# A graph layer that lives on gathers: idle writes on GpSimd behind every twentieth gather, a longer ring and shorter terms

## Chip, cores and metric

The kernel runs on one core of one Trainium2 chip. The metric is the device time of one execution in microseconds. Five engines run their own queues: TensorE (PE, with its weight loads as PEld), VectorE (DVE), ScalarE (ACT), GpSimd (POOL) and SyncE (SP, which only issues transfers here).

## What is computed

Two relational graph layers over 50,000 nodes of 128 features and 850,000 edges sorted by destination (16 relations, 8 bases), then a residual and a layer norm. 50,000 of the edges are each node's own loop edge.

```python
def _rgcn_layer(h, src, dst, rel, basis, w_comp, loop_w, bias):
    W = jnp.einsum('rb,bio->rio', w_comp, basis)
    seg = dst * N_REL + rel
    agg = segment_sum(h[src], seg, num_segments=N_ENT * N_REL).reshape(N_ENT, N_REL, -1)
    msg = jnp.einsum('nri,rio->no', agg, W)
    return jax.nn.relu(msg + h @ loop_w + bias)

h = _rgcn_layer(x, src, dst, rel, basis1, w_comp1, loop_w1, bias1)
h = _rgcn_layer(h, src, dst, rel, basis2, w_comp2, loop_w2, bias2)
out = layernorm(x + h)
```

## The kernel before

**Tiles and chunks.** At the start of the first layer the edges are closed up into 800,000 real edges (the loop edges are taken out and handled apart) and cut into 6250 tiles of 128. Ten tiles are a chunk (K = 10), so a layer has 625 chunks (C). Each tile needs 128 rows of h, one for each edge. GpSimd fetches them with one indirect transfer, `gather` (L178), into one of `RING * PER` = 30 places `g0` to `g29`; `row_of(t)` says which one, `fetch` issues five at a time, 30 tiles ahead of their use. The second layer gathers from `H1`, which the first layer has written.

**On TensorE**, a tile's rows are multiplied (L982) by `hot`, a 128x96 matrix that VectorE makes (L872): it sorts the edges of the tile into 12 nearby destinations and weighs them for the 8 bases. Five tiles share a PSUM bank `pa`; ScalarE copies it (L998) into `aT`. The second to last product of five carries the wait for the fifth gather. Four chunks later `aT` is multiplied by the bases (L741), turned, spread over four neighbours (L724) and added into the nodes' sums with `own` masks (L764, L785).

**Weights.** `hot` needs for each edge its relation's 8 coefficients. `weights(c)` makes them for chunks c and c + 1 together: `told_apart` compares relations (every fourth chunk), `summed_over` multiplies (L596) into `terms`, a sum over the 16 relations (L625) goes to the PSUM tile `fixed`. The generator has two steps for a pair of chunks; `beside` takes one step behind the tile t = 5 and one behind t = 8 of every even chunk. `loop_weights` does the same for the loop edges of four groups of nodes (L658).

**Order.** The order on PE, GpSimd, VectorE and ScalarE is written out by hand: the loop over chunks issues products, gathers and copies, and `beside` puts steps of the other work between the ten tiles of a chunk. The iotas of the kernel before (L134, L204, L223, L230 at the start, L521 at the end of the first layer's gathers) make tables of counted columns. L355 and L410 are indirect scatters of the tables of edges, also on GpSimd, in the first layer.

Of the kernel before, what the change touches and what calls it, by code (L numbers as in the profile page):

```python
# [39 lines left out]
F32 = mybir.dt.float32  # L40
# [5 lines left out]
OP = mybir.AluOpType  # L46
AX = mybir.AxisListType
# [3 lines left out]
P = 128  # L51
# [3 lines left out]
K = P // WN  # L55
# [10 lines left out]
Q = AT // 2  # L66
BANK = 512
WEIGHTS = AT * PER * 8
BITS_AT_ONCE = BANK - WEIGHTS
RING = 6  # L70
J = 4
NEAR = 128
BATCH = 4
# [10 lines left out]
def tile_rgcn_resnorm(  # L84
# [15 lines left out]
    nc = tc.nc  # L100
    N, D = x.shape
    NR, NB = w_comp1.shape
    E = edges.shape[1] // 3
    R, M = -(-E // RUN), E - N
    C = -(-M // (K * P))
# [25 lines left out]
    consts = ctx.enter_context(tc.tile_pool(name="consts", bufs=1))  # L131
# [45 lines left out]
    def gather(to, of, idx):  # L177
        return nc.gpsimd.indirect_dma_start(  # L178
            out=to, out_offset=None, in_=of, in_offset=bass.IndirectOffsetOnAxis(ap=idx, axis=0)
        )  # L180
# [11 lines left out]
        return bass.AP(tensor=edges.tensor, offset=edges.offset + j * E + first, ap=ap)  # L192


    rows = [consts.tile([P, D], F32, name=f"g{i}") for i in range(RING * PER)]
    src = consts.tile([P, 2 * C * HALF], I32, name="src")
    key = consts.tile([P, 2 * C * HALF], U8, name="key")
# [371 lines left out]
    def chunked():  # L569
        with (  # L570
# [5 lines left out]
            def ks(c):  # L576
                return min(K, -(-M // P) - c * K)
# [14 lines left out]

            def summed_over(kinds, k):

                terms = hp.tile([P, 2 * K, NB, NR], F32, name="terms", bufs=1)[:, :k]
                nc.vector.tensor_tensor(  # L596
                    terms,
                    kinds[:, :, None, :].to_broadcast([P, k, NB, NR]),
                    table[:, None, :, :].to_broadcast([P, k, NB, NR]),
                    op=OP.mult,  # L600
                )
                return terms

            def told_apart(of, by, width, c, name):

                k = sum(ks(i) for i in range(c, min(c + Q, C)))
                apart = hp.tile([P, Q * K, width], U8, name=name, bufs=1)[:, :k]
                nc.vector.tensor_tensor(
                    apart,
                    of[:, None, :width].to_broadcast([P, k, width]),  # L610
                    by[:, c * K : c * K + k, None].to_broadcast([P, k, width]),
                    op=OP.is_equal,
                )
                return apart

            def weights(c):

                if c % Q == 0:
                    kinds_of[0] = told_apart(of_rel, rel, NR, c, "kinds")
                at = c % Q * K  # L620
                k = ks(c) + (ks(c + 1) if c + 1 < C else 0)
                terms = summed_over(kinds_of[0][:, at : at + k], k)
                yield
                pm = fixed[:, : 2 * K * NB].rearrange("p (k b) -> p k b", b=NB)
                nc.vector.tensor_reduce(pm[:, :k], terms, AX.X, OP.add)  # L625
                weighed_for[c] = pm[:, :K]
                weighed_for[c + 1] = pm[:, K:]
                yield

            def loop_weights(g, n):  # L630

                few = min(T, NGR - g)
                which_rel = hp.tile([P, 2, T, J], I32, name="lrel", bufs=1)
                for h in range(2):
                    nc.sync.dma_start(
                        which_rel[:, h, :few, :],
                        bass.AP(
                            tensor=LREL.tensor,
                            offset=LREL.offset + h * NL + g * GN,
                            ap=[[J, P], [GN, few], [1, J]],  # L640
                        ),
                    )
                yield
                both = hp.tile([P, 2, T * J, NR], U8, name="both_kinds", bufs=1)
                for h in range(2):
                    nc.vector.tensor_tensor(
                        both[:, h, : few * J],
                        of_rel[:, None, 1 : NR + 1].to_broadcast([P, few * J, NR]),
                        which_rel[:, h].rearrange("p t j -> p (t j)")[:, : few * J, None].to_broadcast([P, few * J, NR]),
                        op=OP.is_equal,  # L650
                    )
                nc.vector.tensor_tensor(
                    both[:, 0, : few * J], both[:, 0, : few * J], both[:, 1, : few * J], op=OP.add
                )
                yield
                terms = summed_over(both[:, 0, : few * J], few * J)
                lw = hp.tile([P, T * J, NB], F32, name="lw")
                nc.vector.tensor_reduce(lw[:, : few * J], terms, AX.X, OP.add)  # L658
                yield lw.rearrange("p (t j) b -> p j t b", t=T)

            def from_itself(g, of, n):
# [157 lines left out]
            def done(steps):  # L819
                for _ in steps:  # L820
                    pass
# [38 lines left out]
            for n, of in enumerate((x, H1)):  # L860

                weighed_for, kinds_of, own_of = {}, [None], [None]
# [22 lines left out]
                def added_in(c):  # L885

                    if c < ALONE:
                        return [c - LAG] if c >= LAG else []
                    at = ALONE - LAG + 2 * (c - ALONE)
                    return list(range(at, min(at + 2, C)))  # L890
# [14 lines left out]
                def add(c):  # L905

                    for g in to_nodes(c, n):
                        assert made[0] > g
                        ending.append(finish(g, n))

                def beside(t, c, owning, summing, weighing):

                    if c % 2 == 0 and t in (5, 8):
                        next(weighing, None)
                    if t in (4, 9) or c >= ALONE - 3 and t in (0, 2):
                        next(owning, None)
                    if c < ALONE:
                        if t in (1, 3, 6, 9):
                            next(summing, None)
                    elif c == ALONE:  # L920
                        for _ in range(2):
                            next(summing, None)
                    elif t == (1 if c == C - 1 else 2):
                        done(summing)
                    if t in (2, 6, 9) and ending:
                        if next(ending[0], 0) == 0:
                            ending.pop(0)
                    if t == (4 if c == C - 1 else 5 if c == ALONE else 8):
                        for one in added_in(c):
                            add(one)  # L930
# [3 lines left out]
                def row_of(t):  # L934

                    turn, k = divmod(n * tiles + t, RING * PER)
                    return rows[k if turn % 2 == 0 else k // PER * PER + PER - 1 - k % PER]

                def fetch(some):

                    for t in some:
                        if t < tiles:
                            fetched[t] = gather(row_of(t), of, src[:, t : t + 1]).ins

                fetched = {}
                now, made = [0], [0]
                owning = own_of_all()
                for c in range(C):
# [6 lines left out]
                    if c == 0:  # L955
                        fetch(range(RING * PER))
                        nc.vector.tensor_copy(table, COMP[n].rearrange("p r b -> p b r"))
                        weighing = weights(0)
                        done(weighing)
                        hots[0] = hot_of(0)  # L960
                        hots[1] = hot_of(1)
                        if n == 0:
                            for _ in range(LBITS + 3):
                                next(first_runs)
                    if c % 2 == 0 and c + 2 < C:
                        weighing = weights(c + 2)
# [9 lines left out]
                    for k in range(0, K, PER):  # L976
                        m = min(PER, ks(c) - k)
                        if m > 0:
                            pa = ps_a.tile([P, BANK], F32, name="pa")
                        for i in range(PER):  # L980
# [12 lines left out]
                            if i == m - 1:  # L993
                                at = c * K + k + RING * PER
                                fetch(range(at, at + PER))
# [28 lines left out]
    def summed():  # L1024
        L1 = dram.tile([N, D], F32, name="L1")
        L2 = dram.tile([N, D], F32, name="L2")
        with tc.tile_pool(name="io", bufs=2) as io, tc.tile_pool(name="sbf", bufs=2) as sb:
# [140 lines left out]
            nodes(L2, norm, also=x)  # L1168

    chunked()  # L1170
    wrong = nc.values_load(bad[0:1, 0:1], min_val=0, max_val=1)
    with tc.If(wrong > 0):
# [7 lines left out]
def build(arrays):  # L1180
    import concourse.bacc as _bacc

    nc = _bacc.Bacc("TRN2", target_bir_lowering=False, num_devices=1)
    args = [
        nc.dram_tensor(name, a.shape, mybir.dt.from_np(a.dtype), kind="ExternalInput").ap()
        for name, a in arrays.items()
    ]
    args.append(nc.dram_tensor("out_0_dram", arrays["in_x_dram"].shape, F32, kind="ExternalOutput").ap())
    with tile.TileContext(nc) as tc:
        tile_rgcn_resnorm(tc, *args)  # L1190
    return nc
# [21 lines left out]
```

## Times and profile before

| | |
|---|---|
| median of 3 runs | 15732.13 us (15731.26 to 15733.83) |
| profiled execution, its own time | 15732.04 us |
| its span, from the first to the last instruction | 15730.2 us |
| mean granted TensorE clock | 0.816 |
| busy: PE, DVE, ACT, POOL | 74%, 65%, 12%, 75% of the span |
| gathers | 12,500, two layers of 6250 |

The span is what the trace covers; the time of an execution is 1.8 us more. A row of a group gives the line, the engine, the operation and its tiles (out<-in) with shapes, then the count, the busy time in all (us) and the mean of one (ns), and behind the last bar the idle time of that engine just before them with what ended it. "issue" means that the engine waited for nothing that the profile shows.

### The profile page before, as it was taken

The page shows a single profiled execution, that of the slowest core. Times are in us where ns is not written, and L with a number is a line of the kernel's source. Part 1 is how long each engine was busy: PE and PEld are TensorE (multiplying, and loading weights), DVE is VectorE, ACT ScalarE, POOL GpSimd, SP SyncE. Part 2 cuts the span into 40 slices and gives each one's busy share as a digit, 9 for nine tenths or more (in the row PEclk, how much of TensorE's full clock was granted, in tenths as well). Part 3 has the DMA queues.
Part 4 walks back from the last instruction along what each step waited for, and adds up shares of the span by engine and source line. Part 5 has one row for each costly group of instructions (what it writes and reads, how often), then busy time and mean ns, then how long its engine had stood idle before and what let it go on. Part 6 is the DMA issues. An engine that isn't in the chain of part 4 may idle for free.

```text
span 15730.2 us, 119374 instructions
## 1 busy us (share of the span) xinstructions
PE 11573.8 (74%) x41202; PEld 7067.3 (45%) x41202; DVE 10159.2 (65%) x10480; ACT 1936.8 (12%) x3683; POOL 11853.5 (75%) x12532
## 2 busy tenths in 40 slices
PE   6777777777777777777777777777777777777777
PEld 4444444444444444444444444444444444444444
DVE  8767776777655566556666666666666666666666
ACT  1111111111111111111111111111111111111111
POOL 7777777777777777777777777777777777777777
PEclk8888888888888888888878888888888888878888
DMA  2222222222222222222222222222222222222222
GB/s 83 71 71 67 72 65 71 68 67 70 62 60 60 60 60 60 60 60 60 60 58 64 62 63 62 63 63 63 63 63 63 63 62 63 63 63 63 62 63 61
DMA packets 539213, 1004.82 MB, mean 64 GB/s; under 512 B 261489, under 2 KB 264561, under 8 KB 538612
## 3 DMA queue, kind: packets, MB, share of 16 engines
q0 software_dynamic: 401872, 826.89, 18.4%
q1 hardware_dynamic: 133652, 168.42, 3.4%
q8 instruction: 343, 5.62, 0.1%
q14 instruction: 258, 2.11, 0.0%
q10 hardware_dynamic: 3088, 1.79, 0.0%
HBM read 924.65 MB, written 71.59 MB: 63 GB/s over the span
## 4 chain that ended last, share of the span: by engine, by line
POOL 21%; DMA 11%; issue 10%; PE 8%; DVE 0%; POOLq 0%; ACT 0%; DVEq 0%
POOL g L178 21%; DMA g<-H,src 11%; PE pn L785 3%; PE po L741 3%; PE pa L982 1%; PE po L691 1%; DVE ls L706 0%; PE po L713 0%; PE pn L795 0%; DVE by L698 0%; DVE slots L724 0%; DVE fixed L625 0%; POOLq L178 0%; DVE hot L872 0%; DVE terms L596 0%
## 5 line engine op out<-in xcount | busy, mean ns | idle before, releaser
L982 PE MATMUL pa<-hot,g 128*128 128x96 f32 x25000 | 4897.9, 314 | 4005.0 <-DMA g<-in_x_dram,src 1947.1
L178 POOL DMA_INDIRECT g<-in_x_dram,src x6250 | 5927.2, 948 | 1912.2 <-issue 1643.2
L178 POOL DMA_INDIRECT g<-H,src x6250 | 5902.0, 944 | 1918.5 <-issue 1650.9
L982 PEld LDWEIGHTS pa<-hot,g 128*128 128x128 f32 x25000 | 4305.7, 222 | 6622.5 <-issue 4200.4
L698 DVE TENSOR_TENSOR by<-po,lw 128x512 f32<-128x512 f32 x1568 | 1074.8, 686 | 3926.2 <-PE po L691 3925.4
L785 PE MATMUL pn<-slots,own 120*128 120x512 f32 x4128 | 3193.6, 908 | 63.4 <-DVE own L764 35.0
L998 ACT COPY aT<-pa 128x480 f32<-128x480 f32 x2500 | 1393.6, 557 | 10593.6 <-PE pa L982 10592.0
L741 PE MATMUL po<-aT,basis 128*128 128x480 f32 x4960 | 2162.0, 591 | 0.0
L691 PE MATMUL po<-basis,hT 128*128 128x512 f32 x3136 | 1991.6, 722 | 19.4 <-DVE by L698 16.0
L625 DVE TENSOR_REDUCE fixed<-terms 128x160 f32<-128x2560 f32 x626 | 1764.2, 2818 | 10.2
L596 DVE TENSOR_TENSOR terms<-kinds,fixed 128x2560 f32<-128x2560 uint8 x626 | 1760.0, 2812 | 11.1
L706 DVE TENSOR_REDUCE ls<-by 128x128 f32<-128x1152 f32 (+1 forms) x784 | 1660.3, 2118 | 32.9
L872 DVE TENSOR_TENSOR hot<-fixed,own 128x960 f32<-128x960 f32 x1250 | 1437.8, 1150 | 33.3 <-PE pa L982 16.5
L741 PEld LDWEIGHTS po<-aT,basis 128*128 128x128 f32 x4960 | 966.3, 200 | 984.9 <-issue 984.9
L785 PEld LDWEIGHTS pn<-slots,own 120*128 120x128 f32 x4128 | 1022.6, 278 | 766.8 <-issue 691.3
L724 DVE TENSOR_TENSOR slots<-po,which 120x1024 f32<-120x1024 f32 (+1 forms) x630 | 761.7, 1209 | 541.1 <-PE po L750 513.2
L691 PEld LDWEIGHTS po<-basis,hT 128*128 128x128 f32 x3136 | 581.7, 231 | 25.1 <-DVE by L698 16.9
L745 ACT COPY by_slot<-po 128x480 f32<-128x480 f32 x310 | 173.0, 558 | 2545.1 <-PE po L741 2545.1
L764 DVE TENSOR_SCALAR own<-col,node 120x256 f32<-120x256 f32 (+1 forms) x1250 | 438.1, 351 | 8.1 <-PE pn L785 8.1
L807 DVE TENSOR_TENSOR pn<-pn,ls 128x512 f32<-128x512 f32 x98 | 68.0, 694 | 477.2 <-PE pn L785 477.2
L795 PEld LDWEIGHTS pn<-loop,hT 128*128 128x128 f32 x1568 | 294.9, 262 | 169.3 <-issue 169.3
L807 DVE TENSOR_TENSOR ls<-pn,ls 128x512 f32<-128x512 f32 x98 | 67.2, 685 | 403.4 <-PE pn L785 403.4
(137 smaller groups left out, 3185.4 us busy)
## 6 DMA issues: line engine op xcount, KB each, us to landing
g<-in_x_dram,src POOLq DMA_INDIRECT x6250, 2.5
g<-H,src POOLq DMA_INDIRECT x6250, 2.5
h_own<-in_x_dram SPq DMA_DIRECT2D x97, 256.0 KB, 2.7
xw<-in_x_dram SPq DMA_DIRECT2D x97, 256.0 KB, 2.7
H<-ls SPq DMA_DIRECT2D x97, 256.0 KB, 2.1
h_own<-H SPq DMA_DIRECT2D x97, 256.0 KB, 2.7
out_dram<-ls SPq DMA_DIRECT2D x97, 256.0 KB, 2.4
FULL<-full SPq DMA_DIRECT2D x20, 640.0 KB, 4.5
```

Source lines behind the costliest of these rows:

```text
L178: return nc.gpsimd.indirect_dma_start(out=to, out_offset=None, in_=of, in_offset=bass.IndirectOffsetOnAxis(ap=idx, axis=0))
L596: nc.vector.tensor_tensor(terms, kinds[:, :, None, :].to_broadcast([P, k, NB, NR]), table[:, None, :, :].to_broadcast([P, k, NB, NR]), op= ...
L625: nc.vector.tensor_reduce(pm[:, :k], terms, AX.X, OP.add)
L691: nc.tensor.matmul(hb[:m], hT[:, j, :m], BASIS[n][:, b : b + few, :].rearrange("p b d -> p (b d)"), start=True, stop=True,)
L698: nc.vector.tensor_tensor(by[:m, b : b + few, :], hb[:m].rearrange("p (b d) -> p b d", d=D), lw[:m, j, g % T, b : b + few, None].to_broadc ...
L706: nc.vector.tensor_reduce(ls[:m, j, :], by[:m].rearrange("p b d -> p d b"), AX.X, OP.add)
L724: nc.vector.tensor_tensor(to[:k], of[:k, :, None, :].to_broadcast([k, pair, J, D]), which[:k, c : c + pair, :, None].to_broadcast([k, pair ...
L741: nc.tensor.matmul(ps[:, : BATCH * S], BASIS[n][:, b, :], aT[:, b, :], start=b == 0, stop=b == NB - 1)
L785: nc.tensor.matmul(sums[g], own, of[:k].rearrange("s j d -> s (j d)"), start=c == first(g), stop=c == final(g),)
L872: nc.vector.tensor_tensor(hot[:, : ks(c)], pm[:, : ks(c), :, None].to_broadcast([P, ks(c), NB, WN]), own[:, : ks(c), None, :].to_broadcast ...
L982: product = nc.tensor.matmul(pa[:, i * NB * WN : (i + 1) * NB * WN], row_of(c * K + k + i), hot[:, k + i].rearrange("e b w -> e (b w)"), s ...
L998: nc.scalar.copy(aT[:, :, place_of + k * WN : place_of + (k + m) * WN].rearrange("d b (i w) -> d i b w", w=WN), pa[:, : m * NB * WN].rearr ...
```

## The change

Four edits. Behind every twentieth gather of a layer (t + 1 divisible by 2K) GpSimd writes the counted columns 0 to 639 twice into `lull`, a tile of 128x640 that nothing reads. The ring has 7 x 5 = 35 places, so gathers are issued 35 tiles ahead. `weights` makes product and sum for each chunk of a pair alone, in four steps, and `beside` takes a step behind t = 5 and t = 8 of every chunk. `terms` is half as wide, and `loop_weights` goes through its 16 rows in pieces of ten and six. In SBUF, `lull` (2560 bytes a partition) and five more places (2560 bytes) stand against half of `terms` (5120 bytes).

```diff
-RING = 6
+RING = 7
+IDLE = 640
...
+    lull = consts.tile([P, IDLE], F32, name="lull")
     rows = [consts.tile([P, D], F32, name=f"g{i}") for i in range(RING * PER)]
...
-                terms = hp.tile([P, 2 * K, NB, NR], F32, name="terms", bufs=1)[:, :k]
+                terms = hp.tile([P, K, NB, NR], F32, name="terms", bufs=1)[:, :k]
...
-                at = c % Q * K
-                k = ks(c) + (ks(c + 1) if c + 1 < C else 0)
-                terms = summed_over(kinds_of[0][:, at : at + k], k)
-                yield
                 pm = fixed[:, : 2 * K * NB].rearrange("p (k b) -> p k b", b=NB)
-                nc.vector.tensor_reduce(pm[:, :k], terms, AX.X, OP.add)
-                weighed_for[c] = pm[:, :K]
-                weighed_for[c + 1] = pm[:, K:]
-                yield
+                for i in range(c, min(c + 2, C)):
+                    at, to = i % Q * K, pm[:, (i - c) * K : (i - c + 1) * K]
+                    terms = summed_over(kinds_of[0][:, at : at + ks(i)], ks(i))
+                    yield
+                    nc.vector.tensor_reduce(to[:, : ks(i)], terms, AX.X, OP.add)
+                    weighed_for[i] = to
+                    yield
...
-                terms = summed_over(both[:, 0, : few * J], few * J)
                 lw = hp.tile([P, T * J, NB], F32, name="lw")
-                nc.vector.tensor_reduce(lw[:, : few * J], terms, AX.X, OP.add)
+                for k in range(0, few * J, K):
+                    m = min(K, few * J - k)
+                    terms = summed_over(both[:, 0, k : k + m], m)
+                    nc.vector.tensor_reduce(lw[:, k : k + m], terms, AX.X, OP.add)
...
-                    if c % 2 == 0 and t in (5, 8):
+                    if t in (5, 8):
                         next(weighing, None)
...
                             fetched[t] = gather(row_of(t), of, src[:, t : t + 1]).ins
+                            if (t + 1) % (2 * K) == 0:
+                                for _ in range(2):
+                                    nc.gpsimd.iota(
+                                        lull,
+                                        pattern=[[1, IDLE]],
+                                        base=0,
+                                        channel_multiplier=0,
+                                        allow_small_or_imprecise_dtypes=True,
+                                    )
```

## The prediction

> **What bounds the kernel now.** I read the page first (engine totals, the chain, the groups), then GpSimd's own waits, then its timeline where something interrupts its stream. Columns of a group: count, then busy us and mean ns of one, then idle time before them and what ended it.
>
> ```profile
> span 15730.2 us, 119374 instructions
> PE 11573.8 (74%) x41202; PEld 7067.3 (45%) x41202; DVE 10159.2 (65%) x10480; ACT 1936.8 (12%) x3683; POOL 11853.5 (75%) x12532
> POOL 21%; DMA 11%; issue 10%; PE 8%; DVE 0%; POOLq 0%; ACT 0%; DVEq 0%
> L982 PE MATMUL pa<-hot,g 128*128 128x96 f32 x25000 | 4897.9, 314 | 4005.0 <-DMA g<-in_x_dram,src 1947.1
> L178 POOL DMA_INDIRECT g<-in_x_dram,src x6250 | 5927.2, 948 | 1912.2 <-issue 1643.2
> L178 POOL DMA_INDIRECT g<-H,src x6250 | 5902.0, 944 | 1918.5 <-issue 1650.9
> ```
>
> No engine is above 75% and the chain splits over four names, so the shares alone name no limit. The two L178 rows do. Busy and idle together, the 12,500 gathers fill 5927.2 + 1912.2 + 5902.0 + 1918.5 = 15659.9 us of the 15730.2. What is that idle time? GpSimd's waits (total us, times, longest us):
>
> ```profile
> POOL g L178 <- issue: 3294.1, 10764, 14.0
> POOL g L178 <- DMA g<-in_x_dram,src: 189.3, 621, 0.3
> POOL g L178 <- DMA g<-H,src: 184.7, 606, 0.3
> POOL g L178 <- PE pa L982: 101.5, 333, 0.3
> ```
>
> Whatever is named, a wait is 0.3 us: 189.3/621 = 0.305, 101.5/333 = 0.305, and (3294.1 - 14.0)/10763 = 0.305. It is a constant step between two gathers, and the releaser is only whatever happened to occur inside it; the chain's "DMA" and "issue" are partly this step too. So a gather costs 0.944 + 0.305 = 1.249 us, and 12,500 of them 15,613 us. That is the kernel: GpSimd never waits for a free place nor for TensorE, while TensorE waits for gathers. The rest is the start, the step between the layers and the tail. GpSimd's timeline at the step between the layers (start, duration, in brackets the idle time before):
>
> ```profile
> 7886.79 0.94 POOL L178 DMA_INDIRECT g<-in_x_dram,src  x1 [0.30 <-issue]
> 7887.75 0.65 POOL L521 IOTA even<- 1x625 f32 x1
> 7902.45 0.95 POOL L178 DMA_INDIRECT g<-H,src  x1 [14.05 <-issue]
> 7903.70 0.95 POOL L178 DMA_INDIRECT g<-H,src  x1 [0.30 <-issue]
> 7904.96 0.94 POOL L178 DMA_INDIRECT g<-H,src  x1 [0.30 <-issue]
> 7906.20 0.94 POOL L178 DMA_INDIRECT g<-H,src  x1 [0.30 <-issue]
> ```
>
> Two things are to be seen. An iota queued behind a gather starts when that gather ends (7886.79 + 0.94 = 7887.73, start 7887.75): it does not run beside it. And after a pause of 14 us the gathers go on at 1.25 us each: rest is not paid back by a faster pace.
>
> **The change, part by part.**
>
> *The lulls.* A layer has 6250 gathers; the condition holds at every 20th, so 312 times a layer, 624 times in all, with 1248 iotas of 128x640. The trace has iotas of nearby sizes, alone and one behind the other at the start:
>
> ```profile
> L223 POOL IOTA place<- 128x672 f32 x1 | 0.7, 687 | 0.0
> L521 POOL IOTA even<- 1x625 f32 x1 | 0.7, 652 | 0.0
> L204 POOL IOTA col<- 128x256 f32 x1 | 0.3, 334 | 0.0
> ```
> ```profile
> 1.52 0.69 POOL L223 IOTA place<- 128x672 f32 x1
> 2.17 0.40 POOL L230 IOTA spread<- 5x120 f32 x2
> ```
>
> A column costs (687 - 334)/(672 - 256) = 0.849 ns, so 640 columns cost 687 - 32 x 0.849 = 660 ns. L521, met in the middle of the gathers, gives 652 + 15 x 0.849 = 665, so gathers before it do not slow an iota. An iota behind an iota starts 2.17 - 1.52 = 0.65 us after it, 0.04 ahead of its recorded end. A lull then lasts, from the end of its gather, 0.02 + (0.66 - 0.04) + 0.66 = 1.30 us.
>
> What comes after is not in the trace: no gather follows an iota without a wait for something else. Either the 0.30 us step still stands between the last iota and the next gather, and the lull adds 1.30 + 0.30 - 0.30 = 1.30 us; or the step runs under the iotas, and it adds 1.00. Below that I see no way: the iotas themselves have to run. The nearest row is an indirect transfer that was released by VectorE after GpSimd had been idle for 18 us:
>
> ```profile
> 19.66 0.89 DVE L353 SCALAR_TENSOR_TENSOR full<-both,run_first,real 128x640 f32<-128x640 f32 x1
> 20.84 1.14 POOL L355 DMA_INDIRECT FULL<-full,to_i  x1 [18.27 <-DVE full L353]
> ```
>
> Its release is at 19.66 + 0.89 = 20.55 and it starts 0.29 us later, though the engine had had all the time to prepare it. So the step comes after whatever lets the instruction go, and should come after an iota too; since a successor can start 0.04 us ahead of an iota's recorded end, I take 0.26 to 0.30, that is 1.26 to 1.30, and 1.28 as the value. 624 x 1.28 = 799 us. With the step hidden it is 624 x 1.00 = 624 us.
>
> All of it lies on the path: the stream of gathers has no slack in which a lull could lie, and the last lulls of each layer stand 10 gathers before its end. Behind a lull are queued the next gathers, in the first layer also the few scatters of the run tables; TensorE waits for the gathers.
>
> *35 places.* A gather may run 35 instead of 30 ahead. No wait of GpSimd above 0.305 us was for a place, so this takes nothing off: 0. Should a lull let TensorE fall behind, the five places are cover, not gain. At the very start five more gathers stand before the first scatter of the loop relations, 5 x 1.25 = 6 us and one lull more; that delays VectorE once, not GpSimd.
>
> *Terms for single chunks.* One product and one sum over 2560 columns become two of each over 1280. Both shapes are in the trace, since the last chunk has no partner:
>
> ```profile
> L625 DVE TENSOR_REDUCE fixed<-terms 128x160 f32<-128x2560 f32 x624 | 1761.2, 2822 | 10.2
> L596 DVE TENSOR_TENSOR terms<-kinds,fixed 128x2560 f32<-128x2560 uint8 x624 | 1757.0, 2816 | 11.0
> L625 DVE TENSOR_REDUCE fixed<-terms 128x80 f32<-128x1280 f32 x2 | 3.0, 1495 | 0.1
> L596 DVE TENSOR_TENSOR terms<-kinds,fixed 128x1280 f32<-128x1280 uint8 x2 | 3.0, 1486 | 0.1
> ```
>
> The pair costs 2 x 1486 - 2816 = 156 ns and 2 x 1495 - 2822 = 168 ns more, together 324 ns x 624 = 202 us of VectorE; the loop's terms, 48 of 2048 columns now cut in two, add some 15 us by the same step. VectorE is busy 10159 of 15730 us, and two chunks (20 gathers, 25 us) hold 16 us of its work, so 0.35 us more is hidden by its idle time, and the work is spread more evenly over odd and even chunks. Without that cover it would be 217 us. A weight is now finished one chunk before its use is prepared instead of two, in the same chunk as the product that needs it and ahead of it in VectorE's order: 0.
>
> *Sum.* The profiled execution took 15732.04 us with its span of 15730.2; the median of the three runs, 15732.13, is the same. 15732 + 799 = **16531 us**, 5.1% more.
>
> **A rule weighed.** The transfers themselves, by the page's queues and issues:
>
> ```profile
> q0 software_dynamic: 401872, 826.89, 18.4%
> g<-H,src POOLq DMA_INDIRECT x6250, 2.5
> ```
>
> A gather lands 2.5 us after its issue, two gathers' distance, and the queue takes 18.4% of the transfer engines: nothing piles up there, and the pace is that of GpSimd's own instructions. The Trainium skill, DMA: Bandwidth & Descriptors, section Anatomy of one DMA, puts most of the fixed 2 us of such a transfer on completion and calls the generation of descriptors small; by that rule issuing would not be the limit and the time would stay. The rows do not bear it out for a stream of gathers: 1.249 us of each are GpSimd's.
>
> A second rule speaks for more than my sum. VectorE's masks beside a gather:
>
> ```profile
> 9178.53 0.35 DVE L764 TENSOR_SCALAR own<-col,node 120x256 f32<-120x256 f32 x1
> 9178.67 1.02 POOL L178 DMA_INDIRECT g<-H,src  x1 [0.30 <-issue]
> 9179.99 0.94 POOL L178 DMA_INDIRECT g<-H,src  x1 [0.30 <-issue]
> ```
>
> This gather took 1.02 instead of 0.94 us. It is rare: the second layer's mean is 944 ns, that of an undisturbed gather. The Trainium skill, SBUF — State Buffer, section Who interferes with whom, says that a VectorE instruction in a two-port mode and a GpSimd instruction exclude each other for their whole length. Which mode L764 runs in the trace does not say.
>
> **The rivals.**
>
> *The step is hidden.* GpSimd prepares the next gather under the iotas. For it: its sequencer reads ahead while a gather runs, as an iota's immediate start shows. Against it: the 0.29 us after a release. 15732 + 624 = 16356 us.
>
> *VectorE holds up the iotas.* A lull comes once per two chunks, as regularly as VectorE's masks, and an iota writes all the time it runs. If every lull met one L764 and lost the 0.35 us of the row above, 624 x 0.35 = 218 us come on top: 16749 us. Against it: the gathers' mean.
>
> *Not slower.* The lulls are absorbed, because what paces the gathers is not GpSimd but the transfers behind it, with the 1.249 us as back-pressure, or because the unread writes are dropped from the program. Its price is 0, so 15732 us; it decides if the pace after a pause is quicker until some 1.3 us are made up. Against it: the pace after the 14 us pause, the landing after 2.5 us, and a step equal to a hundredth of a microsecond throughout. For a gain over 0.2% (31 us, about what a measurement of this kernel can tell from no change) I find no place at all: but for the start and the step between the layers, every wait is the constant 0.3 us.
>
> **How the numbers follow.** The forecast 0.72, the hidden step 0.15, VectorE's hold 0.09, not slower 0.04. The first two lie between 16356 and 16543; the range 16340 to 16680 takes in these and the milder half of the third. Slower 0.96; same 0.03; faster 0.01.
>
> **What would show it.** Right: 1248 iotas of about 660 ns on GpSimd, the first 0.02 us behind its gather, the second 0.62 behind the first; gathers still at 0.944 with 0.305; GpSimd's sum of gathers, iotas and steps still some 99.5% of the span; TensorE's idle time before L982 up by about what the span grows. The gap between the second iota and the next gather tells forecast (0.26 to 0.30) from hidden step (about 0). Iotas with a mean well above 0.70 us speak for VectorE's hold. Wrong: gathers behind a lull that are shorter or closer than 1.249 us, or a real wait of GpSimd for a place.

## The result, and the profile after

The changed kernel takes 16570.81 us (median of 4 runs, 16568.65 to 16571.33) against 15732.98 us before: 837.8 us more, a ratio of 1.0533 (95% interval 1.052 to 1.0546). The profiled execution took 16571.33 us, its span is 16569.5 us. From its page (totals, chain, groups):

```profile
span 16569.5 us, 122045 instructions
PE 12051.0 (73%) x41202; PEld 7356.0 (44%) x41202; DVE 10397.1 (63%) x11824; ACT 1937.3 (12%) x3683; POOL 12705.1 (77%) x13780
POOL 29%; issue 12%; DMA 5%; PE 4%; POOLq 0%; DVE 0%; ACT 0%; DVEq 0%
L994 PE MATMUL pa<-hot,g 128*128 128x96 f32 x25000 | 5127.5, 325 | 4376.1 <-DMA g<-H,src 2146.1
L179 POOL DMA_INDIRECT g<-in_x_dram,src x6250 | 5927.5, 948 | 1883.0 <-issue 1740.1
L179 POOL DMA_INDIRECT g<-H,src x6250 | 5904.9, 945 | 1888.3 <-issue 1752.7
L949 POOL IOTA lull<- 128x640 f32 x1248 | 848.7, 680 | 47.6
```

The gathers are what they were (L179 is L178 of before): 0.3 and 2.9 us more of busy time in 5900. New is the row L949, 1248 iotas, which with the idle time ahead of them fill 896 us. The gathers' own idle time has fallen from 3830.7 to 3771.3 us. So 848.7 + 47.6 + 3.2 - 59.4 = 840.1 us on GpSimd, and the span grew by 839.3: all of it is GpSimd's time. TensorE waited longer for gathers, 4376 instead of 4005 us, and its own work took longer too (busy 12051.0 instead of 11573.8 us, at a granted clock of 0.787 instead of 0.816). The chain's shares moved toward GpSimd, but as before they do not add up to its part.

One lull on GpSimd's timeline (the two iotas are merged into one row), and one of a rarer kind:

```profile
8027.46 0.95 POOL L179 DMA_INDIRECT g<-in_x_dram,src  x1 [0.30 <-issue]
8028.71 0.94 POOL L179 DMA_INDIRECT g<-in_x_dram,src  x1 [0.30 <-issue]
8029.66 1.41 POOL L949 IOTA lull<- 128x640 f32 x2
8031.23 0.95 POOL L179 DMA_INDIRECT g<-in_x_dram,src  x1 [0.15 <-issue]
8032.48 0.95 POOL L179 DMA_INDIRECT g<-in_x_dram,src  x1 [0.30 <-issue]
...
7579.64 0.94 POOL L179 DMA_INDIRECT g<-in_x_dram,src  x1 [0.30 <-issue]
7580.58 1.50 POOL L949 IOTA lull<- 128x640 f32 x2
7584.71 0.95 POOL L179 DMA_INDIRECT g<-in_x_dram,src  x1 [2.63 <-issue]
```

A lull is 1.41 us of iotas and then 0.15 us, half of the step between two gathers, until the next gather starts. Worked out over all 624 lulls of the trace (means): the first iota starts 0.008 us behind the gather, the second 0.763 us behind the first (0.694 us of iota and 0.069 of idle time), lasts 0.666 us, and the next gather starts 0.189 us later (0.153 in nearly all, 2.63 in nine). That is 1.626 us where a step of 0.305 stood: 1.321 us x 624 = 824 us. Most of the other 14 us are fourteen steps between gathers of 0.4 to 2.0 us, of which the trace of before has none.

### The profile page after: what moved, and what is told of

The parts are those of the page before. It is cut to its first block, busy times and chain, and to the rows that moved or that the text cites. A ratio compares the mean times of both kernels' runs of the same rounds, so it can differ in the third digit from the quotient of the medians.

```text
span 16569.5 us, 122045 instructions
## 1 busy us (share of the span) xinstructions
PE 12051.0 (73%) x41202; PEld 7356.0 (44%) x41202; DVE 10397.1 (63%) x11824; ACT 1937.3 (12%) x3683; POOL 12705.1 (77%) x13780
## 4 chain that ended last, share of the span: by engine, by line
POOL 29%; issue 12%; DMA 5%; PE 4%; POOLq 0%; DVE 0%; ACT 0%; DVEq 0%
POOL g L179 27%; DMA g<-H,src 5%; POOL lull L949 2%; PE po L744 1%; PE pn L788 1%; PE pa L994 1%; PE po L694 0%; PE pn L798 0%; POOLq L179 0%; PE po L716 0%; ACT ls L569 0%; DVE pn L810 0%; DVE st L558 0%; DVE mv L559 0%; DVE slots L727 0%
## 5 line engine op out<-in xcount | busy, mean ns | idle before, releaser
L994 PE MATMUL pa<-hot,g 128*128 128x96 f32 x25000 | 5127.5, 325 | 4376.1 <-DMA g<-H,src 2146.1
L994 PEld LDWEIGHTS pa<-hot,g 128*128 128x128 f32 x25000 | 4495.0, 231 | 7090.0 <-issue 4593.1
L179 POOL DMA_INDIRECT g<-in_x_dram,src x6250 | 5927.5, 948 | 1883.0 <-issue 1740.1
L179 POOL DMA_INDIRECT g<-H,src x6250 | 5904.9, 945 | 1888.3 <-issue 1752.7
L788 PE MATMUL pn<-slots,own 120*128 120x512 f32 x4128 | 3105.7, 886 | 45.6 <-DVE own L767 26.1
L744 PE MATMUL po<-aT,basis 128*128 128x480 f32 x4960 | 2368.5, 637 | 0.0
L694 PE MATMUL po<-basis,hT 128*128 128x512 f32 x3136 | 2104.7, 760 | 16.8 <-DVE by L701 15.6
L627 DVE TENSOR_REDUCE fixed<-terms 128x80 f32<-128x1280 f32 x1250 | 1864.6, 1492 | 30.4
L598 DVE TENSOR_TENSOR terms<-kinds,fixed 128x1280 f32<-128x1280 uint8 x1250 | 1849.1, 1479 | 12.1
L744 PEld LDWEIGHTS po<-aT,basis 128*128 128x128 f32 x4960 | 1062.9, 221 | 1105.1 <-issue 1105.1
L949 POOL IOTA lull<- 128x640 f32 x1248 | 848.7, 680 | 47.6
L767 DVE TENSOR_SCALAR own<-col,node 120x256 f32<-120x256 f32 (+1 forms) x1250 | 489.4, 392 | 16.9 <-PE pn L788 16.9
```

Source lines behind the costliest of these rows:

```text
L179: return nc.gpsimd.indirect_dma_start(out=to, out_offset=None, in_=of, in_offset=bass.IndirectOffsetOnAxis(ap=idx, axis=0))
L598: nc.vector.tensor_tensor(terms, kinds[:, :, None, :].to_broadcast([P, k, NB, NR]), table[:, None, :, :].to_broadcast([P, k, NB, NR]), op= ...
L627: nc.vector.tensor_reduce(to[:, : ks(i)], terms, AX.X, OP.add)
L694: nc.tensor.matmul(hb[:m], hT[:, j, :m], BASIS[n][:, b : b + few, :].rearrange("p b d -> p (b d)"), start=True, stop=True,)
L744: nc.tensor.matmul(ps[:, : BATCH * S], BASIS[n][:, b, :], aT[:, b, :], start=b == 0, stop=b == NB - 1)
L788: nc.tensor.matmul(sums[g], own, of[:k].rearrange("s j d -> s (j d)"), start=c == first(g), stop=c == final(g),)
```

## The experiments

Theory: a lull costs GpSimd's own time for it, in series with the gathers, and the rest of the change costs nothing. Rivals: the break of the stream costs, whatever its length; the longer ring or the split terms carry a part; VectorE holds up the iotas. Each run was timed against the kernel before on the same chip.

**The lulls taken away, the rest kept.** Edit: the loop over iotas and the tile `lull` removed.

> The changed kernel without the idle iotas: 35 places and terms for single chunks stay. If the lulls are the whole of the change, it takes what the kernel before took, 15733 us within 0.2% (31 us), with gathers every 1.249 us. Rival: if the split terms or the longer ring carry part of the 838 us, it stays above 15765 us; the split terms alone could give at most their 217 us of VectorE, that is 15950 us.

Measured: 15733.81 us, ratio 0.9997 (0.9988 to 1.0007). The groups of gathers:

```profile
L179 POOL DMA_INDIRECT g<-in_x_dram,src x6250 | 5929.2, 949 | 1911.8 <-issue 1769.3 <-DMA g<-in_x_dram,src 60.6 <-PE pa L984 48.8
L179 POOL DMA_INDIRECT g<-H,src x6250 | 5905.2, 945 | 1916.9 <-issue 1785.0 <-PE pa L984 56.4 <-DMA g<-H,src 52.4
```

Busy and idle time together, this is the stream of before to within 3 us a layer. 35 places and terms for single chunks cost and bring nothing that can be measured; the lulls are the whole change.

**Half a lull.** Edit: `for _ in range(1):` in place of `range(2)`.

> One iota of 640 columns behind every twentieth gather instead of two. Theory (a lull costs the engine time of its iotas, less the part of the gathers' step that lies under them): 0.01 + 0.69 + 0.15 - 0.305 = 0.55 us x 624 = 340 us, with the rare long steps of the changed kernel (about 35 us) some 16075 to 16110 us. Rival (a break of the stream of gathers costs the same however long it is): 16571 us. Rival (the lulls are partly made up): below 16000 us.

Measured: 16087.52 us, ratio 1.0221 (1.0204 to 1.0238), 350 us more than the kernel before beside it (15737.86). That is 0.56 us a lull, against 1.34 with two iotas: the price follows what GpSimd has to do, the break alone is not it. It is less than half, which the next runs explain. The range given had counted 35 us of long steps; this kernel has none, and its lull is a little dearer than forecast (0.56 instead of 0.55 us).

**One iota twice as often.** Nearly the same number of iotas, 1250 instead of 1248:

```diff
-if (t + 1) % (2 * K) == 0:
-    for _ in range(2):
+if (t + 1) % K == 0:
+    for _ in range(1):
```

> The same 1248 iotas of 640 columns, but one behind every tenth gather instead of two behind every twentieth. Theory: each costs 0.01 + 0.68 + 0.15 - 0.305 = 0.54 us, 1248 x 0.54 = 670 us, with no wait between two iotas and the 0.15 us of the step saved twice as often: 16400 to 16450 us. Rival (only the iotas' number and length count): 16571 us. Rival (each break costs the 1.34 us of a lull): 17400 us.

Measured: 16440.36 us, ratio 1.0447 (1.043 to 1.0465), 706 us more than 15734.41. Nearly equal work, 130 us less than in pairs. The iotas' row:

```profile
L949 POOL IOTA lull<- 128x640 f32 x1250 | 862.9, 690 | 8.9
```

The wait between two iotas is gone (8.9 instead of 47.6 us of idle time ahead of the iotas), the step of the next gather is shortened by half 1250 times instead of 624, and the long steps are gone as well.

**A tile for each iota of a lull.**

```diff
-RING = 7
+RING = 6
-    lull = consts.tile([P, IDLE], F32, name="lull")
+    lulls = [consts.tile([P, IDLE], F32, name=f"lull{i}") for i in range(2)]
...
-                                for _ in range(2):
+                                for lull in lulls:
```

> The changed kernel with a tile of its own for each of the two iotas of a lull, and with 30 places again (the room of the five places goes to the second tile). In the changed kernel the second iota starts 0.07 us after the recorded end of the first; at the start of the kernel before, an iota into another tile started 0.04 us ahead of that end. Theory: the second iota waits for the first because both write one tile. Then 0.11 us x 624 = 67 us go away: 16504 us, gap between the iotas -0.04 us. Rival: the gap belongs to two long iotas, and the time stays at 16571 us. If the five places are needed as cover against the lulls, it gets slower than 16571 us and GpSimd shows waits of more than 0.31 us for TensorE.

Measured: 16480.56 us, ratio 1.0472 (1.0454 to 1.0489); 743 us more than the kernel before beside it, where the changed kernel had 838. A lull, the iotas, and GpSimd's waits for TensorE:

```profile
8038.46 0.94 POOL L179 DMA_INDIRECT g<-in_x_dram,src  x1 [0.30 <-issue]
8039.41 1.30 POOL L949 IOTA lull<- 128x640 f32 x2
8040.87 0.95 POOL L179 DMA_INDIRECT g<-in_x_dram,src  x1 [0.16 <-issue]
```
```profile
L949 POOL IOTA lull<- 128x640 f32 x1248 | 823.2, 691 | 4.3
```
```profile
POOL g L179 <- PE pa L994: 46.6, 153, 0.3
POOL g L179 <- PE po L694: 32.6, 108, 0.3
```

The pair takes 1.30 instead of 1.41 us, and of 47.6 us of idle time ahead of the iotas 4.3 are left: the second iota had been waiting for the first, which writes the same tile. (In both traces the iotas carry a wait for a semaphore that the iotas themselves raise; with one tile only the first of all has none, with two the first into each tile. So with one tile it is the iota just ahead that is waited for, with two one of the lull before.) Over all lulls the second now starts 0.620 instead of 0.763 us behind the first, but lasts 0.033 us longer. The long steps of 0.4 to 2.6 us are gone too, which had not been expected and is the main reason why the time lies below the expected 16504 us. 30 places are enough: no gather waits longer than 0.3 us for TensorE.

**Other masks.** VectorE's masks no longer by tensor_scalar:

```diff
-nc.vector.tensor_scalar(own, columns, node4[:k, c : c + 1], float(-some[0] * GN),
-    op0=OP.subtract, op1=OP.is_equal)
+nc.vector.scalar_tensor_tensor(own, columns, float(some[0] * GN),
+    node4[:k, c : c + 1, None].to_broadcast([k, len(some), P]), op0=OP.add, op1=OP.is_equal)
```

> The changed kernel with VectorE's masks made by scalar_tensor_tensor (column plus the group's first node, compared with the node) instead of tensor_scalar; same result. If tensor_scalar's mode is what holds up the iotas now and then, the means of the two iotas fall from 694 and 666 ns to their medians of some 680 and 664, about 10 us in all: 16560 us; the masks themselves no longer vary in length. Rival (VectorE's hold is a main part of the lulls' price): below 16450 us. Rival (the masks have nothing to do with it): 16571 us and the same means.

Measured: 16587.33 us, ratio 1.0539 (1.0522 to 1.0557). By its time it cannot be told from the changed kernel, whose 1.0533 lies inside the interval; the trace shows two effects of opposite sign. The groups of the gathers and iotas:

```profile
L179 POOL DMA_INDIRECT g<-in_x_dram,src x6250 | 5941.9, 951 | 1882.7 <-issue 1795.3 <-DMA g<-in_x_dram,src 34.7 <-PE pa L994 21.5
L179 POOL DMA_INDIRECT g<-H,src x6250 | 5919.0, 947 | 1885.6 <-issue 1806.1 <-DMA g<-H,src 33.5 <-PE pa L994 28.8
L949 POOL IOTA lull<- 128x640 f32 x1248 | 841.1, 674 | 47.3
```

The iotas got 7.6 us shorter (about 10 were expected): the first of a lull fell from a mean of 0.694 to 0.683 us. What had not been expected, and puts the time above the expected 16560 us: the gathers got 28 us longer. The two traces show that it is the masks. In the changed kernel 144 first iotas overlap a mask and take 0.733 us on the mean, the others 0.682; with the new masks both take 0.683. The mask pays more than the iota: one of 120x256 takes 0.64 us where it overlaps an iota and 0.37 elsewhere, a new one 0.42 in either place. And of the gathers' 28 us some 24 lie in gathers that overlap a mask. VectorE and GpSimd do hold each other up, but that is worth 8 us on the lulls, not 218. The Trainium skill, SBUF — State Buffer, section Who interferes with whom, says that a VectorE instruction with two SBUF inputs is in the way of a GpSimd instruction that reads SBUF, not of one that only writes it; both signs here agree, since the new masks have two SBUF inputs (`col4` and `node4`), a gather reads its row numbers from the SBUF tile `src`, and an iota only writes.

**Short iotas.** Edit: `IDLE = 64`.

> Two iotas of 64 columns instead of 640 behind every twentieth gather: the same number of instructions, waits and breaks, a tenth of the columns. Theory (columns at 0.849 ns are engine time on the path): 2 x 576 x 0.849 ns = 0.98 us less a lull, 610 us in all: about 15960 us. Rival (the break of the stream costs, not its length): 16571 us.

Measured: 16197.96 us, ratio 1.0295 (1.0278 to 1.0312), 464 us more than 15734.41. Both expectations missed: the price fell, but by 374 us, not by 610. The timeline shows where the rest stayed:

```profile
8007.15 0.94 POOL L179 DMA_INDIRECT g<-in_x_dram,src  x1 [0.30 <-issue]
8008.10 0.46 POOL L949 IOTA lull<- 128x64 f32 x2
8009.09 0.95 POOL L179 DMA_INDIRECT g<-in_x_dram,src  x1 [0.53 <-issue]
8010.34 0.95 POOL L179 DMA_INDIRECT g<-in_x_dram,src  x1 [0.30 <-issue]
```

The iotas shrank to 0.46 us, but the step after them grew from 0.15 to 0.53. In 609 of 623 lulls the gather starts 0.71 to 0.73 us behind the start of the second iota, whether that lasts 0.18 or 0.36 us. That suggested a new theory: preparing a gather takes GpSimd 0.71 us, as a rule hidden under the instruction ahead, and an iota that waits holds it back. The last run was made to test it.

**Short iotas, a tile for each.** Edit: both of the above, `IDLE = 64` and two tiles with 30 places.

> Two iotas of 64 columns behind every twentieth gather, each into a tile of its own (30 places). With one tile the next gather started 0.71 us after the start of the second iota, 0.53 us after its end. Theory: GpSimd needs 0.71 us to prepare a gather, normally under the instruction before; an iota that waits for the one before it holds the preparation back until it goes. Without the wait the gather follows 0.16 us behind the iota's end, as behind the long ones, the rare steps of 1.2 and 2.6 us go away too, and a lull adds 0.01 + 0.20 + 0.13 + 0.16 - 0.305 = 0.2 us: about 15735 + 125 = 15860 us. Rival (the preparation begins only when the instruction ahead starts, wait or not): a lull adds 0.01 + 0.14 + 0.71 - 0.305 = 0.56 us: about 16080 us. Rival (the place behind an iota costs the same for short ones as with one tile): 16198 us.

Measured: 15859.89 us, ratio 1.0081 (1.0064 to 1.0097). The theory's number was 15860.

```profile
8017.86 0.95 POOL L179 DMA_INDIRECT g<-H,src  x1 [0.30 <-issue]
8018.81 0.34 POOL L949 IOTA lull<- 128x64 f32 x2
8019.31 0.95 POOL L179 DMA_INDIRECT g<-H,src  x1 [0.15 <-issue]
8020.56 0.95 POOL L179 DMA_INDIRECT g<-H,src  x1 [0.30 <-issue]
```

Without the wait the gather follows 0.15 us behind the iotas again, and beside the start and the step between the layers none is longer than 0.32 us. The rival by which preparation begins only with the instruction ahead (16080 us) falls. That the time agrees to a tenth of a microsecond is luck; the test is between 15860, 16080 and 16198 us.

The queue's own records in the traces show the holding back. Before every fifth gather GpSimd's queue has a separate semaphore check (EVENT_SEMAPHORE), for the semaphore that this gather's transfer then uses. In the kernel before, GpSimd makes this check 7.5 us ahead of its gather (median of 2496), five or six instructions early: it reads far ahead. With two tiles it goes on doing so across a lull (8.6 us ahead with long iotas, 7.6 with short ones). With one tile the check for the gather behind a lull comes only 0.04 us after the end of the first iota, just before the second starts (622 of 624 lulls), and the gather starts 0.84 us after the check with long iotas and 0.74 us with short ones. So an iota that waits stops the reading of everything behind it. But for one lull, no gather then starts sooner than some 0.71 us after the start of that iota; what GpSimd does in this time is not shown, "preparation" is a name for it.

None of these beats the kernel before; the nearest, the kernel without lulls, equals it.

## Why the prediction held, and which terms were off

**What bounds the kernel**: right. The stream of gathers is a series of 1.249 us steps, and the span grew by what was put into it, to within 1 us. Nothing was absorbed, so the rival "not slower" is out. With it goes, for this stream of gathers, what the prediction had weighed as a rule: that issuing is small beside completion (the Trainium skill, DMA: Bandwidth & Descriptors, section Anatomy of one DMA) and so would not be the limit. Transfers still land after 2.5 us, and every added stretch of GpSimd's time shows in the span.

**Nothing from the ring and the terms**: right, shown by the kernel without lulls. VectorE's terms (L627, L598) take 3713.7 us, 189.5 more than before (202 were forecast), hidden.

**The price of a lull**: 799 us forecast, 838 measured, but two of the steps behind the 1.28 us were wrong and nearly cancelled, which is luck.

- An iota behind an iota was to start 0.04 us ahead of its recorded end. The row that this came from had two different tiles. Here both iotas write one tile, the second waits, and it starts 0.07 us behind that end. 0.11 us x 624 = 68 us too little. The diff showed the single tile; the wait could have been foreseen from it.
- "So the step comes after whatever lets the instruction go, and should come after an iota too". It is 0.153 us behind an iota, not 0.26 to 0.30: half of it is gone, as if it ran under the iota, so the rival "hidden step" was half right. Some 0.13 us x 624 = 79 us too much. The row chosen for it, a transfer released by another engine, was the wrong neighbour.
- The iotas: 0.694 and 0.666 us against 0.66 each, 25 us too little. VectorE's masks account for 8 of them; that rival had the right mechanism at a small price.
- The nine steps of 2.63 us and the fourteen of up to 2.0 us between gathers, some 36 us, were in no row of before.
- The first iota starts 0.008 instead of 0.02 us behind its gather: 7 us too much. The step that a lull replaces is 0.305, not 0.30 us: 3 us too much.

68 - 79 + 25 + 36 - 7 - 3 = 40 us, against 39 measured. The range held because it spanned both ends of the unknown step, not because the value in it was right.

**A sign that did not come.** TensorE's idle time before its products was to rise by about what the span grows, 839 us. It rose by 371 (4005.0 to 4376.1). TensorE's own busy time rose by 477 us (11573.8 to 12051.0), at a granted clock of 0.787 instead of 0.816, and took up the rest of the longer span. The prediction had counted no change of TensorE's own work; as TensorE only waits for gathers, the time does not show it.

**Open.** The long steps occur in the three timed kernels in which an iota waits for another (the changed one, other masks, short iotas with one tile), and in none of the six others, the kernel before among them. They come at the same gathers in all three (the short iotas have one more), every 1060 gathers over long stretches. GpSimd's waits put some of them down to TensorE:

```profile
POOL g L179 <- PE pa L994: 48.4, 144, 2.6
```

That would be the wait for a place that the prediction names as a sign of being wrong. It is none: in all nine lulls that have such a step the gather starts 3.29 us behind the start of the second iota, with 640 columns and with 64, and a wait for TensorE would not be so constant. That the long steps belong to the waiting iotas is shown; what they are is not.

## What to carry to other kernels

Where one engine's idle time is the same 0.3 us whatever releases it, it is part of each instruction: count the instructions, and expect work added to that queue to show in the time; here all of it did but half a step for each break. When pricing an added instruction, look for its own waits first: here two writes of one unread tile were still ordered, and the wait also held back what stood behind it, by 0.38 us a lull with short iotas. An estimate that comes out right can hide two wrong terms; measuring each term in the trace and changing one at a time found both.

## What was not expected of the hardware

- A gather starts 0.305 us behind a gather but 0.15 to 0.16 us behind an iota, and not earlier than about 0.71 us after an iota that had to wait has started (short iotas: 0.53 us of idle time with the wait, 0.15 without).
- GpSimd reads its queue 7.5 us ahead of a gather, and an iota that waits ends this lead: behind it 0.74 to 0.84 us are left.
- VectorE's masks with two SBUF inputs left the iotas alone (0.683 us beside a mask and elsewhere) and made the gathers 28 us longer in all than tensor_scalar did; tensor_scalar cost the iotas 8 us, and its masks went from 0.37 to 0.64 us beside an iota.
- The granted TensorE clock fell from 0.816 to 0.787 in the changed kernel, although TensorE idled more ahead of its products; it was 0.815 without lulls and 0.801 with half of them. As TensorE only waits for gathers, the time shows nothing of it, and its cause was not tried.
